# Layer 3's cross attention: query weights multiplied into the context's keys, scores taken straight from the tokens

## The chip, the cores and the metric

The kernel runs on one core of one Trainium2 chip. The metric is the device time of one launch in microseconds (us). The core has a matrix engine (TensorE, "PE" in the profile, with its weight loads as "PEld"), a vector engine (VectorE, "DVE"), a scalar engine (ScalarE, "ACT"), a general engine (GpSimd, "POOL") and an engine that issues most DMAs (SyncE, "SP"). Six runs of the kernel before took 2142.23 to 2151.93 us, median 2146.32 us.

## The reference, cut to what matters

A decoder of four layers; each layer adds self attention, cross attention to a short context, and a feed-forward block with experts to the tokens `x` (4 batches, 512 tokens, width 128), each on the layer-normed tokens. The context `ctx_1024` has 77 rows of width 128 in each of the 4 batches and is the same in all layers. The change is in the cross attention of the last layer, which has 16 heads of 64:

```python
def _L3_xattn_ref(query, key, value, w_q, w_k, w_v, w_o):
    HEADS = 16
    HEAD_DIM = 64
    scale = HEAD_DIM ** (-0.5)
    q = (query @ w_q).reshape(B, Q, HEADS, HEAD_DIM).transpose(0, 2, 1, 3)
    k = (key @ w_k).reshape(B, Kl, HEADS, HEAD_DIM).transpose(0, 2, 1, 3)
    v = (value @ w_v).reshape(B, Kl, HEADS, HEAD_DIM).transpose(0, 2, 1, 3)
    scores = jnp.einsum('bhqd,bhkd->bhqk', q, k) * scale
    attn = jax.nn.softmax(scores, axis=-1)
    out = jnp.einsum('bhqk,bhkd->bhqd', attn, v)
    out = out.transpose(0, 2, 1, 3).reshape(B, Q, HEADS * HEAD_DIM)
    return out @ w_o

x = x + _L3_xattn_ref(_layernorm(x), ctx_1024, ctx_1024, L3_xattn_w_q, L3_xattn_w_k, L3_xattn_w_v, L3_xattn_w_o)
x = x + _L3_ffn_ref(_layernorm(x), ...)
```

The weights `w_q`, `w_k` and `w_v` are 128 x 1024 and `w_o` is 1024 x 128. All products are in f32.

## The kernel before, in words

The tokens stay on chip all the time: `x` by rows (16 tiles of 128 tokens x 128), and `xT`, the normed tokens turned (128 x 2048), of which `tokens(b)` is a batch's 512 columns and `tile_of(t)` one tile's 128 columns. The stages follow one another, and beside the experts of a layer (much matrix work) the attention of the next is worked on: `weave(dense, chain, every)` writes the steps of a generator `dense` and after each `every` of them one step of a generator `chain`. What is written first has priority. A planner then sets, when the kernel is built, the order of each engine's instructions from its own cost model; engines named in `manual_schedule` keep the written order. Queues run in that order, each engine waiting for the semaphores of its own next instruction. Each f32 product shows as two matrix instructions in the trace, a transpose as one.

Cross attention of layer 3 has three parts.

*The context's part*, `l3_context` (L2215), depends on no token and is worked out early, in turns (`turns`, L408) with the second half of layer 0's experts (`ffn("l0_ffn", second, ...)`, 18 steps), while the chain beside them does layer 1's attention for batches 0 and 1 and its router (66 steps, one for each 0.48 dense steps, after a lead of 3). `l3_context` has 17 steps: one that loads the weights for keys, values and output (512 KB each, pool `x3c`), then two for each of eight pairs of heads `hp`. The first computes the pair's keys (128 x 308: two heads of 64 on the partitions, 4 x 77 context rows) and its values, each in a PSUM bank of the tag `f` (four banks, shared with the experts) and copied out by ACT; two DMAs store the keys in DRAM (`kd`). The second multiplies the values by `w_o`, head by head, and stores 77 x 512 for each head (`vd`). So values carry `w_o` already.

*The fetch*, `l3_keys` (L2246), is called inside the end of layer 3's self attention (`last`, L2109, where the order on PE, DVE, ACT and POOL is the written one). It clears a tile `kb` of 128 x (8 pairs, 4 batches, 2 heads, 77) with a POOL memset, since the two heads of a pair must not mix, and loads each head's keys into its own 64 partitions; the other 64 stay zero. It also loads the values `vo`.

*The main part*, `l3_xattn` (L2260), runs over 32 items (batch b, pair hp) in four phases, written one after the other with lags of 0, 1, 4 and 3 items (`lagged`, L418): `projections` (the pair's queries for the batch's 512 tokens, copied out by ACT with the factor 0.125), `scores`, `values`, `turn`. `scores` makes two PSUM tiles of one bank each, for two token tiles each: for a token tile it multiplies the 128 queries by the pair's keys with their zeros, 154 columns. Then for each of the two tiles: maximum, subtraction, sum and reciprocal on DVE, `exp` on ACT, and the multiplication by the reciprocals on POOL. `turn` transposes finished blocks of 128 (head, row) columns (10 blocks for the 8 pairs, 4 transposes each), ACT copies them out, and `values` multiplies each by `vo` into the batch's sum. PSUM banks: five of the tag `mm` (queries, scores and transposes take turns), two `acc`, one `s`.

Beside it the chain does the norms of batches 1 to 3 and, for batches 0, 1 and 2 in turn, `add_columns`, the norm and the router of layer 3's experts (`route_slots`, L759). POOL keeps the written order here: after each of POOL's multiplications in `scores`, `put` (L807) issues a waiting indirect DMA that sends 128 tokens to their expert's slots; for batch 3's items the second multiplication is followed by two. 16 such puts belong to each of three batches. What is left of them is put after the items, and the slots' experts follow.

The query weights come through `feed`, the list of weight packs that are loaded one after the other into four slots (`want`, `pack`): the pack `l3_xattn.q` stands between layer 2's experts and layer 3's.

Of the kernel before, what the change touches and what calls it, by code (L numbers as in the profile page):

```python
# [13 lines left out]
F32 = mybir.dt.float32  # L14
# [8 lines left out]
P = 128  # L23
B, S, D = 4, 512, 128
NT = B * S // P
TB = S // P
L = 77
# [103 lines left out]
def pack_all(inp):  # L131
    f32 = np.float32
    packs = {}


    p = packs["const"] = Pack()
# [15 lines left out]
    c, s = np.cos(ang).astype(f32), np.sin(ang).astype(f32)  # L152
# [5 lines left out]
    p = packs["l0_attn.qk"] = Pack()  # L158
    w, bias = inp["L0_attn_W_attn"], inp["L0_attn_b_attn"]
# [6 lines left out]
    p = packs["l0_attn.vo"] = Pack()  # L166
# [88 lines left out]
    for n in ("Wq", "Wk", "Wv"):  # L255
        p.add(n, inp["L3_attn_" + n].T)

    for n in "kvq":
        packs[f"l3_xattn.{n}"] = Pack()
        packs[f"l3_xattn.{n}"].add(n, inp["L3_xattn_w_" + n])  # L260
    packs["l3_xattn.o"] = Pack()
    packs["l3_xattn.o"].add("o", inp["L3_xattn_w_o"].reshape(8, P, D).transpose(1, 0, 2))

    p = packs["s5"] = Pack()
    p.add("gate_bias", rep(inp["L3_ffn_bias"]))
# [24 lines left out]
class Net:  # L290
# [1924 lines left out]
    def l3_context(self, pool):  # L2215

        nc = self.nc
        Wk, Wv, Wo = (self.load("l3_xattn." + n, pool, "x3" + n) for n in "kvo")
        kd = self.away.tile([2, 64, 8, B, L], F32, name="x3_k")
        vd = self.away.tile([16 * L, B, D], F32, name="x3_vo")  # L2220
        self.x3 = kd, vd
        yield
        for hp in range(8):
            c = slice(hp * P, hp * P + P)
            pk = self.bank("f", (P, B, L))
            self.dot(pk.rearrange("p b l -> p (b l)"), (Wk["k"][:, c], self.const["ctxT"]))
            k = pool.tile([P, B, L], F32, tag="x3kT", name="x3kT", bufs=2)
            nc.scalar.copy(k, pk)
            for h in range(2):
                nc.sync.dma_start(kd[h, :, hp], k[64 * h : 64 * h + 64])  # L2230
            pv = self.bank("f", (P, B * L))
            self.dot(pv, (Wv["v"][:, c], self.const["ctxT"]))
            vT = pool.tile([P, B * L], F32, tag="x3vT", name="x3vT", bufs=2)
            nc.scalar.copy(vT, pv)
            yield
            vo = pool.tile([L, 2, B, D], F32, tag="x3vo", name="x3vo", bufs=2)
            heads = [(h, slice(64 * h, 64 * h + 64), self.bank("f", (P, B, D))) for h in range(2)]
            for b in range(B):
                for h, r, po in heads:
                    self.dot(po[:L, b, :], (vT[r, b * L : b * L + L], Wo["o"][r, c]))  # L2240
            for h, r, po in heads:
                nc.scalar.copy(vo[:, h], po[:L])
            nc.sync.dma_start(vd[2 * hp * L : 2 * (hp + 1) * L].rearrange("(h l) b d -> l h b d", l=L), vo)
            yield

    def l3_keys(self, pool):  # L2246


        kd, vd = self.x3
        kb = pool.tile([P, 8, B, 2, L], F32, name="kb")  # L2250
# [9 lines left out]
    def l3_xattn(self, base, pool):  # L2260

        nc, tc = self.nc, self.tc
        HP = 8
        Wq = self.pack(base, "l3_xattn.q")
        kb, vo = self.x3
        items = [(b, hp) for b in range(B) for hp in range(HP)]
        made = {}
        accs = {}  # L2270
        rows = [(r, min(r + P, 16 * L)) for r in range(0, 16 * L, P)]

        blocks = [[i for i, (_, r) in enumerate(rows) if (r - 1) // (2 * L) == hp] for hp in range(HP)]

        def projections(b, hp):
            c = slice(hp * P, hp * P + P)
            pq = self.mm()
            self.dot(pq, (Wq["q"][:, c], self.tokens(b)))
            q = pool.tile([P, S], F32, tag="q", name="q", bufs=3)
            nc.scalar.mul(q, pq, 0.125)  # L2280
            made[b, hp, "q"] = q

        def scores(b, hp):
            q = made.pop((b, hp, "q"))
            es = []
            for j0 in range(0, TB, 2):
                s = self.mm((P, 4, L))
                for j in range(2):
                    self.dot(
                        s[:, 2 * j : 2 * j + 2, :].rearrange("p h l -> p (h l)"),  # L2290
                        (q[:, (j0 + j) * P : (j0 + j + 1) * P], kb[:, hp, b].rearrange("p h l -> p (h l)")),
                    )
                es.append(s)
            if hp == 0:
                made[b, "e"] = pool.tile([P, TB, 16, L], F32, tag="heads", name="heads", bufs=2)
            for i, s in enumerate(es):
# [4 lines left out]
                nc.vector.tensor_reduce(m, s, AX.X, ALU.max)  # L2301
                self.tt(e, s, wide(m), ALU.subtract)
                nc.scalar.activation(e, e, AF.Exp)
                nc.vector.tensor_reduce(r, e, AX.X, ALU.add)
                nc.vector.reciprocal(r, r)
                nc.gpsimd.tensor_tensor(e, e, wide(r), ALU.mult)
                if (b, hp) not in items[-2:]:
                    self.put(2 if i and b == B - 1 else 1)

        def turn(b, hp):  # L2310
            e = made[b, "e"].rearrange("p j h l -> p j (h l)")
            for i in blocks[hp]:
                r0, r1 = rows[i]
                t = self.mm((P, TB, P))
                for j in range(TB):
                    nc.tensor.transpose(t[: r1 - r0, j, :], e[:, j, r0:r1], self.ident)
                eT = pool.tile([P, S], F32, tag="eT", name="eT", bufs=4)
                nc.scalar.copy(eT[: r1 - r0], t[: r1 - r0].rearrange("l j q -> l (j q)"))
                made[b, i] = eT

        def values(b, hp):
            if hp == 0:
                accs[b] = self.acc()
            for i in blocks[hp]:
                n = rows[i][1] - rows[i][0]
                nc.tensor.matmul(  # L2326
                    accs[b], lhsT=vo[:n, i, b, :], rhs=made.pop((b, i))[:n], start=i == 0, stop=i == len(rows) - 1,
                )
# [24 lines left out]

def build(nc, packs, dram):
# [9 lines left out]
    at = {}  # L2364
    for name, part in (
        ("l0a", of("l0_ffn")), ("l0b", of("l0_ffn")), ("l1a", of("l1_ffn")), ("l1b", of("l1_ffn")),
        ("l2", f2 + one_by_one), ("x3", ["l3_xattn.q"]), ("l3", of("l3_ffn")[:3]),
    ):
        at[name] = len(feed)
        feed += part  # L2370
    with tile.TileContext(nc) as tc, ExitStack() as ctx:
# [102 lines left out]
        close_pool("f2")  # L2474


        net.want(at["x3"])
# [11 lines left out]
        x3 = open_pool("x3")  # L2489
        banks(mm=5, acc=2, s=1)  # L2490
        w5 = net.load("s5", s5, "w")
        steps = net.l3_xattn(at["x3"], x3)

        class Both(dict):
            def __missing__(self, name):
# [66 lines left out]
```

## Time and profile before

| what | value |
|---|---|
| median of six runs | 2146.32 us |
| profiled execution, its own time | 2143.78 us |
| span of its trace | 2142.1 us, mean granted TensorE clock 0.983 |
| PE / DVE / ACT / POOL busy in the span | 95% / 74% / 46% / 28% |
| context's part, first keys to last values stored | 303.7 to 395.8 us |
| main part, first query product to last sum copied out | 1887.5 to 2033.5 us |

A view by lines gives, for a line of the code, an engine and an operation, how many instructions there were and their durations. A view by windows gives for each stretch of time how long each engine was busy, the number of its instructions, the share of full speed that the TensorE clock was granted (PEclk), and the mean busy share of the 16 DMA engines. The chain of waits follows the work that ended last backwards; on it the pitch of matrix instructions can be read, which is shorter than the duration of one, since they are pipelined.

### The profile page before, as it was taken

The page shows a single profiled execution, that of the slowest core. Times are in us where ns is not written, and L with a number is a line of the kernel's source. Part 1 is how long each engine was busy: PE and PEld are TensorE (multiplying, and loading weights), DVE is VectorE, ACT ScalarE, POOL GpSimd, SP SyncE. Part 2 cuts the span into 40 slices and gives each one's busy share as a digit, 9 for nine tenths or more (in the row PEclk, how much of TensorE's full clock was granted, in tenths as well). Part 3 has the DMA queues.
Part 4 walks back from the last instruction along what each step waited for, and adds up shares of the span by engine and source line. Part 5 has one row for each costly group of instructions (what it writes and reads, how often), then busy time and mean ns, then how long its engine had stood idle before and what let it go on. Part 6 is the DMA issues. An engine that isn't in the chain of part 4 may idle for free.

```text
span 2142.1 us, 27766 instructions
## 1 busy us (share of the span) xinstructions
PE 2032.2 (95%) x8804; PEld 1065.9 (50%) x8804; DVE 1593.2 (74%) x3932; ACT 990.1 (46%) x2023; POOL 594.2 (28%) x778
## 2 busy tenths in 40 slices
PE   6989999999999999999999999999999999899886
PEld 3555546554545453444444544444444444466553
DVE  6788675756765779778977798777866877599755
ACT  4556546444325462534543454434433544267541
POOL 2110101000000001433333243332432355145753
PEclk8999999999999999999999999999999999999988
DMA  6421443344453343333333444444454354431112
GB/s 161 122 78 47 107 113 101 93 130 112 116 133 91 90 110 98 86 103 97 104 105 106 111 112 126 123 129 120 125 137 117 99 142 124 96 97 39 32 43 82
DMA packets 93985, 222.56 MB, mean 104 GB/s; under 512 B 22178, under 2 KB 43106, under 8 KB 93582
## 3 DMA queue, kind: packets, MB, share of 16 engines
q1 hardware_dynamic: 90702, 218.63, 37.7%
q0 software_dynamic: 3136, 2.16, 0.4%
q8 instruction: 69, 1.13, 0.2%
q14 instruction: 78, 0.64, 0.1%
HBM read 192.55 MB, written 23.53 MB: 101 GB/s over the span
## 4 chain that ended last, share of the span: by engine, by line
PE 60%; DVE 13%; ACT 3%; issue 3%; POOL 2%; DMA 1%; another core or an unknown queue 0%; SPq 0%; DVEq 0%; POOLq 0%; ACTq 0%
PE mm L431 17%; PE f L431 11%; PE mm L1874 8%; PE s L431 6%; PE mm L1846 5%; PE acc L1039 5%; PE mm L1821 4%; DVE h L442 1%; DVE at_m L1907 1%; ACT at_e L1909 1%; DVE gvx L442 1%; PE acc L2326 1%; DVE k_work L442 1%; DVE og L442 1%; PE acc L1077 1%
## 5 line engine op out<-in xcount | busy, mean ns | idle before, releaser
L1782 POOL TENSOR_TENSOR gvx<-gvx 128x512 f32<-128x512 f32 (+1 forms) x256 | 262.9, 1027 | 529.9 <-DVE gvx L442 471.5
L431 PE MATMUL f<-xT,w_l_ffn 128*128 128x512 f32 (+1 forms) x700 | 334.9, 599 | 1.3 <-ACT h L1031 0.7
L1909 ACT ACTIVATE at_e<-mm,at_m 128x512 f32<-128x512 f32 x256 | 173.1, 686 | 265.0 <-DVE at_m L1907 259.6
L431 PE MATMUL mm<-w_l_ffn_qkv,xT 128*128 128x512 f32 x512 | 264.4, 602 | 3.3 <-DVE gvx L442 1.7
L1874 PE MATMUL mm<-og,w_l_ffn_o 128*128 128x512 f32 x512 | 263.2, 600 | 2.8 <-DVE og L442 1.4
L442 DVE TENSOR_TENSOR h<-h,f 128x512 f32<-128x512 f32 (+1 forms) x175 | 119.5, 685 | 120.7 <-PE f L431 95.9
L1031 ACT ACTIVATE h<-f 128x512 f32<-128x512 f32 x172 | 102.2, 596 | 211.7 <-PE f L431 188.1
L442 DVE TENSOR_TENSOR gvx<-mm,gv 128x512 f32<-128x512 f32 x256 | 174.2, 684 | 23.9 <-PE mm L431 20.0
L442 DVE TENSOR_TENSOR og<-mm,c 128x512 f32<-128x512 f32 x256 | 174.0, 682 | 22.8 <-PE mm L1874 21.0
L431 PEld LDWEIGHTS f<-xT,w_l_ffn 128*128 128x128 f32 (+1 forms) x700 | 125.7, 190 | 130.2 <-issue 107.4
L1039 PE MATMUL acc<-h,w_l_ffn 128*128 128x512 f32 x344 | 176.8, 597 | 4.9 <-DVE h L442 3.6
L1907 DVE TENSOR_REDUCE at_m<-mm 128x1 f32<-128x512 f32 x256 | 161.2, 682 | 11.8 <-PE mm L431 11.2
L1822 ACT COPY eT<-mm 128x512 f32<-128x512 f32 x256 | 137.3, 595 | 68.3 <-PE mm L1821 68.0
L1821 PEld LDWEIGHTS mm<-ident,at_e 128*128 128x128 f32 x1024 | 119.4, 141 | 66.5 <-issue 45.4
L1874 PEld LDWEIGHTS mm<-og,w_l_ffn_o 128*128 128x128 f32 x512 | 91.3, 190 | 114.6 <-issue 90.5
L1821 PE MATMUL mm<-ident,at_e 128*128 128x128 f32 x1024 | 134.7, 273 | 3.3 <-ACT at_e L1909 3.3
L431 PEld LDWEIGHTS mm<-w_l_ffn_qkv,xT 128*128 128x128 f32 x512 | 86.9, 190 | 91.5 <-issue 54.5
L431 PE MATMUL mm<-roped 64*128 64x512 f32 x512 | 129.4, 615 | 1.6 <-DVE roped L442 1.6
L1846 PE MATMUL mm<-eT,v 128*64 128x512 f32 x512 | 118.5, 598 | 2.1 <-ACT eT L1822 2.1
L442 DVE TENSOR_TENSOR h<-h,c 128x512 f32<-128x512 f32 x160 | 111.2, 700 | 3.3 <-DMA c<-l_ffn_w 0.4
L1248 ACT ACTIVATE e<-mm 128x512 f32<-128x512 f32 (+1 forms) x176 | 92.1, 554 | 42.9 <-PE mm L1244 39.0
L1202 DVE TENSOR_REDUCE m<-mm 128x1 f32<-128x512 f32 (+3 forms) x176 | 102.5, 625 | 9.5 <-PE mm L1198 8.8
(528 smaller groups left out, 3485.0 us busy)
## 6 DMA issues: line engine op xcount, KB each, us to landing
c<-gates SPq DMA_DIRECT2D x256, 256.0 KB
c<-l_ffn_w SPq DMA_DIRECT2D x96, 384.0 KB
w_l_ffn_qkv<-in_l_ffn_qkv SPq DMA_DIRECT2D x24, 640.0 KB
w_l_ffn<-in_l_ffn SPq DMA_DIRECT2D x26, 576.0 KB
w_l_ffn_o<-in_l_ffn_o SPq DMA_DIRECT2D x24, 512.0 KB
rot<-qk SPq DMA_DIRECT2D x128, 64.0 KB
d<-inverted SPq DMA_DIRECT2D x64, 128.0 KB
k_parts<-k SPq DMA_DIRECT2D x12, 384.0 KB
```

Source lines behind the costliest of these rows:

```text
L431: self.nc.tensor.matmul(out, lhsT=lhsT, rhs=rhs, start=i == 0, stop=i == len(pairs) - 1)
L442: self.nc.vector.tensor_tensor(out, a, b, op)
L1031: nc.scalar.activation(h, pg, AF.Silu)
L1039: nc.tensor.matmul(acc["t"], lhsT=W["d" + u], rhs=h, start=i == 0, stop=i == n - 1)
L1202: nc.vector.tensor_reduce(m[:, i, h0 : h0 + per], ps, AX.X, ALU.max, negate=True)
L1782: nc.gpsimd.tensor_tensor(x[:, :, :m], x[:, :, :m], x[:, :, m : 2 * m], ALU.add)
L1821: nc.tensor.transpose(p[:, j, :], es[i][hl][:, j * P : j * P + P], self.ident)
L1822: nc.scalar.copy(eT[hl][:, :, i * P : i * P + P], p)
L1846: nc.tensor.matmul(po[64 * hl : 64 * hl + 64, :], lhsT=m["v"][:, j, hl, :], rhs=eT[hl][:, j, :], start=j == 0, stop=j == TB - 1,)
L1874: nc.tensor.matmul(acc, lhsT=W["o"][:, (e - 1) * D : e * D], rhs=hs.pop(e - 1), start=e == 1, stop=e == E)
L1907: nc.vector.tensor_reduce(m, s, AX.X, ALU.max, negate=True)
L1909: nc.scalar.activation(e[:, :n], s, AF.Exp, bias=m, accum_out=den)
```

## The change

Scores are q k^T = x (w_q k^T), so the query weights can be multiplied into the keys, once for all tokens. The change does so in the context's part. The query weights are packed by head dimension (1024 rows in 8 blocks of 128), loaded in `l3_context` between those for keys and values, and no longer in `feed`. The keys are copied out with the factor 0.125; a new step multiplies, for each of the pair's two heads, the head's 64 rows of `w_q` (transposed) by the head's keys (128 x 308 in an `f` bank), ACT copies both into one tile, and one DMA stores them. `l3_context` has 25 steps in place of 17. The stored keys are 128 rows deep for each head and not 64: `kd` and the loads from it move 2.52 MB and not 1.26 MB, in four DMAs of 4,928 bytes a partition and not two of pieces of 308 bytes; the memset is gone. In `l3_xattn` the phase `projections` is gone, `scores` multiplies `tile_of` by `kb`, and the lags and the weave's numbers are set for three phases.

```diff
     def l3_context(self, pool):
-        Wk, Wv, Wo = (self.load("l3_xattn." + n, pool, "x3" + n) for n in "kvo")
-        kd = self.away.tile([2, 64, 8, B, L], F32, name="x3_k")
+        Wk, Wq, Wv, Wo = (self.load("l3_xattn." + n, pool, "x3" + n) for n in "kqvo")
+        kd = self.away.tile([B, P, 8, 2, L], F32, name="x3_k")
...
-            k = pool.tile([P, B, L], F32, tag="x3kT", name="x3kT", bufs=2)
-            nc.scalar.copy(k, pk)
-            for h in range(2):
-                nc.sync.dma_start(kd[h, :, hp], k[64 * h : 64 * h + 64])
+            kT = pool.tile([P, B * L], F32, tag="x3kT", name="x3kT", bufs=2)
+            nc.scalar.mul(kT, pk, 0.125)
...
+            yield
+            k = pool.tile([P, B, 2, L], F32, tag="x3kx", name="x3kx", bufs=2)
+            heads = [(h, slice(64 * h, 64 * h + 64), self.bank("f", (P, B, L))) for h in range(2)]
+            for h, r, pk in heads:
+                self.dot(pk.rearrange("p b l -> p (b l)"), (Wq["q"][r, c], kT[r]))
+            for h, r, pk in heads:
+                nc.scalar.copy(k[:, :, h, :], pk)
+            nc.sync.dma_start(
+                kd[:, :, hp].rearrange("b p h l -> p b (h l)"), k.rearrange("p b h l -> p b (h l)")
+            )
             yield
...
     def l3_keys(self, pool):
-        kb = pool.tile([P, 8, B, 2, L], F32, name="kb")
+        kb = pool.tile([P, B, 8, 2, L], F32, name="kb")
...
-        self.nc.gpsimd.memset(kb, 0.0)
-        for h in range(2):
-            self.nc.sync.dma_start(kb[64 * h : 64 * h + 64, :, :, h, :], kd[h])
+        for b in range(B):
+            self.nc.sync.dma_start(kb[:, b], kd[b])
...
     def l3_xattn(self, pool):
-        def projections(b, hp):
-            c = slice(hp * P, hp * P + P)
-            pq = self.mm()
-            self.dot(pq, (Wq["q"][:, c], self.tokens(b)))
-            q = pool.tile([P, S], F32, tag="q", name="q", bufs=3)
-            nc.scalar.mul(q, pq, 0.125)
-            made[b, hp, "q"] = q
...
-                        (q[:, (j0 + j) * P : (j0 + j + 1) * P], kb[:, hp, b].rearrange("p h l -> p (h l)")),
+                        (self.tile_of(TB * b + j0 + j), kb[:, b, hp].rearrange("p h l -> p (h l)")),
...
-        return self.lagged(items, (projections, 0), (scores, 1), (values, 4), (turn, 3))
+        return self.lagged(items, (scores, 0), (values, 3), (turn, 2))
...
-        ("l2", f2 + one_by_one), ("x3", ["l3_xattn.q"]), ("l3", of("l3_ffn")[:3]),
+        ("l2", f2 + one_by_one), ("l3", of("l3_ffn")[:3]),
...
-            net.weave(some(steps, 40), chained(net.norm(1), net.empty_slots(s5), net.norm(2), net.norm(3)), 2.5)
+            net.weave(some(steps, 28), chained(net.norm(1), net.empty_slots(s5), net.norm(2), net.norm(3)), 1.75)
             w5.gate = net.load("s5.gate", s5, "wg")
-            net.weave(some(steps, 32), chain5(0), 1.3, ahead=300)
+            net.weave(some(steps, 24), chain5(0), 0.97, ahead=300)
             net.want(at["l3"] + 1)
-            net.weave(some(steps, 32), chain5(1), 1.3, ahead=300)
-            net.weave(steps, chain5(2), 0.85, ahead=300)
+            net.weave(some(steps, 24), chain5(1), 0.97, ahead=300)
+            net.weave(steps, chain5(2), 0.71, ahead=300)
```

More of the change, by code (lines that the diff above doesn't have):

```diff
@@ L256, in pack_all @@
         p.add(n, inp["L3_attn_" + n].T)
-    for n in "kvq":
+    for n, w in (
+        ("k", inp["L3_xattn_w_k"]), ("v", inp["L3_xattn_w_v"]),
+        ("q", inp["L3_xattn_w_q"].T.reshape(8, P, D).transpose(1, 0, 2)),
+        ("o", inp["L3_xattn_w_o"].reshape(8, P, D).transpose(1, 0, 2)),
+    ):
         packs[f"l3_xattn.{n}"] = Pack()
-        packs[f"l3_xattn.{n}"].add(n, inp["L3_xattn_w_" + n])
-    packs["l3_xattn.o"] = Pack()
-    packs["l3_xattn.o"].add("o", inp["L3_xattn_w_o"].reshape(8, P, D).transpose(1, 0, 2))
+        packs[f"l3_xattn.{n}"].add(n, w)
     p = packs["s5"] = Pack()
@@ L2224, in l3_context @@
             c = slice(hp * P, hp * P + P)
-            pk = self.bank("f", (P, B, L))
-            self.dot(pk.rearrange("p b l -> p (b l)"), (Wk["k"][:, c], self.const["ctxT"]))
-            k = pool.tile([P, B, L], F32, tag="x3kT", name="x3kT", bufs=2)
-            nc.scalar.copy(k, pk)
-            for h in range(2):
-                nc.sync.dma_start(kd[h, :, hp], k[64 * h : 64 * h + 64])
+            pk = self.bank("f", (P, B * L))
+            self.dot(pk, (Wk["k"][:, c], self.const["ctxT"]))
+            kT = pool.tile([P, B * L], F32, tag="x3kT", name="x3kT", bufs=2)
+            nc.scalar.mul(kT, pk, 0.125)
             pv = self.bank("f", (P, B * L))
@@ L2258, in l3_keys, with l3_xattn @@
         self.x3 = kb, vo
-    def l3_xattn(self, base, pool):
+    def l3_xattn(self, pool):
         nc, tc = self.nc, self.tc
         HP = 8
-        Wq = self.pack(base, "l3_xattn.q")
         kb, vo = self.x3
@@ L2273, in l3_xattn @@
         blocks = [[i for i, (_, r) in enumerate(rows) if (r - 1) // (2 * L) == hp] for hp in range(HP)]
-        def projections(b, hp):
-            c = slice(hp * P, hp * P + P)
-            pq = self.mm()
-            self.dot(pq, (Wq["q"][:, c], self.tokens(b)))
-            q = pool.tile([P, S], F32, tag="q", name="q", bufs=3)
-            nc.scalar.mul(q, pq, 0.125)
-            made[b, hp, "q"] = q
         def scores(b, hp):
-            q = made.pop((b, hp, "q"))
             es = []
@@ L2474, in build @@
         close_pool("f2")
-        net.want(at["x3"])
         x3c, a3b = open_pool("x3c"), open_pool("a3b")
@@ L2491, in build @@
         w5 = net.load("s5", s5, "w")
-        steps = net.l3_xattn(at["x3"], x3)
+        steps = net.l3_xattn(x3)
         class Both(dict):
```

## The prediction

> **What bounds the kernel now.** The change touches two stages, so I read those, first by windows, then for waits. The first table is from layer 0's experts with the context's part beside them, the second from the main part. Columns: stretch, its length, then busy us (and instructions) of PE, PEld, DVE, ACT and POOL, granted clock, DMA share, GB/s.
>
> ```profile
> 320.00:340.00 20.00, 20.00 (x125) 14.66 (x124) 10.48 (x25) 15.73 (x30) 2.75 (x4) 1.00 0.36 100
> ...
> 360.00:380.00 20.00, 19.22 (x116) 13.49 (x115) 10.85 (x41) 8.98 (x18) 1.41 (x2) 1.00 0.18 54
> ```
> ```profile
> 1949.00:1964.00 15.00, 15.00 (x76) 10.13 (x75) 13.89 (x49) 8.58 (x18) 6.27 (x8) 1.00 0.02 6
> ...
> 1994.00:2009.00 15.00, 12.90 (x63) 8.12 (x62) 13.76 (x50) 7.93 (x19) 13.12 (x16) 1.00 0.02 3
> ```
>
> Work is moved into a stage where PE has next to no gap, out of one where PE is full but DVE is over 90% full too, and from 1994 on POOL as well. So PE time added counts in full; PE time removed counts only as far as DVE and POOL let it. The waits of the main part (engine and line, what it waited for: us in all, times, longest) say how far:
>
> ```profile
> DVE fits L724 <- PE s L431: 3.0, 2, 2.8
> DVE sm_s L2304 <- ACT heads L2303: 2.7, 8, 0.5
> ...
> DVE sm_m L2301 <- PE mm L431: 2.1, 4, 0.8
> ...
> DVE x L442 <- PE s L462: 1.8, 2, 1.3
> ```
>
> DVE hardly ever waits for the scores (sm_m, 2.1 us in 146); further down the same answer has 1.1 for the router's sigmoid (sb). For POOL I read its timeline; around an item of batch 3 (start, duration, idle before in brackets):
>
> ```profile
> 2005.45 0.72 POOL L2306 TENSOR_TENSOR heads<-heads,sm_s 128x308 f32<-128x308 f32 x1
> 2006.34 1.00 POOL L801 DMA_INDIRECT slots<-sent,to  x1 [0.17 <-issue]
> 2007.37 0.71 POOL L2306 TENSOR_TENSOR heads<-heads,sm_s 128x308 f32<-128x308 f32 x1
> 2008.25 1.00 POOL L801 DMA_INDIRECT slots<-sent,to  x1 [0.17 <-issue]
> 2009.55 0.97 POOL L801 DMA_INDIRECT slots<-sent,to  x1 [0.30 <-issue]
> ```
>
> From 1995.29 to 2020.75 this pattern (2 multiplications, 3 puts, 5.1 us) runs five times with no idle time but issue gaps: items 25 to 29 go at POOL's pace. Items 17 to 24, one put to a multiplication, take 35.3 us (1960.01 to 1995.29) where 16 x (0.72 + 1.0 + 0.2) = 31 us is POOL's least. Only items 0 to 16 (1893.82 to 1960.01, 3.9 us each) are free of puts.
>
> **What a matrix instruction costs** is its pitch, not its duration. From the chain of waits and PE's timeline:
>
> ```profile
> 1919.29 1.91 PE mm L431 x10
> 1921.20 0.86 PE acc L2326 x2
> 1922.06 0.87 PE mm L2316 x8
> ```
> ```profile
> 389.87 0.68 PE L431 MATMUL f<-w_const,w_l_xattn_k 128*128 128x308 f32 x2
> 390.39 0.68 PE L431 MATMUL f<-w_const,w_l_xattn_v 128*128 128x308 f32 x2
> ...
> 393.58 1.10 PE L431 MATMUL f<-w_l_xattn_o,x3vT 64*77 64x128 f32 x16
> 394.61 3.21 PE L431 MATMUL f<-xT,w_l_ffn 128*128 128x512 f32 x6
> ```
>
> 512 columns: 0.43 us; 308: 0.52 / 2 = 0.26; 128: 0.109; ten with two query instructions: 1.91 - 0.86 = 1.05 for eight of scores. With 64 rows in turns of two heads, 16 of 128 columns start to start in 1.03: 0.064 each, 0.59 of 0.109, so the heads' halves overlap.
>
> **Part 1, the new product in the context's part.** Per pair two products of 64 rows and 308 columns, four instructions, 32 in all. At the full-row pitch: 32 x 0.26 = 8.3 us. If all overlap as the values do: x 0.59 = 4.9. Here a head's two instructions stand together and only the second of one can meet the first of the other: three of four pitches, 8 x 0.78 = **+6.2** (4.9 to 8.3). It lies on PE, with nothing to hide it.
>
> **Part 2, copies, banks and steps.** 16 more ACT copies of 128x308 at 0.416 us (the row of the key copies) = 6.7 us, hidden while ACT is under 80% busy. Each needs an `f` bank until ACT has come; queued behind it on ACT are the experts' silu copies, and PE waits for both. The waits of PE over 300 to 440 us sum to 1.7 us in all, so the margin is thin. The context's steps also outnumber the experts' by more: 25 against 18, and the last seven (2.3 pairs, about 6.6 us of ACT copies) stand alone behind the chain, whose 66 steps end at dense step 35 of 43; layer 1's experts must fill in. I take **+1.5**, between 0 (filled) and 4 (most of the 6.6 seen).
>
> **Part 3, DMAs and queues, costed at 0.** The keys' stores: 8 of 308 KB in pieces of 616 bytes for 16 of 77 KB; DMA is at 0.18 to 0.36 there, SP issues eight fewer. The query weights' load moves from 1811 to about 252 us, ahead of the values' and output's on SP (issued to 262); first use is 303.7, and 512 KB at the 100 GB/s of that stage is 5 us. The memset (4.2 us) leaves POOL, which after it idles 5.4 us for ACT: worth nothing itself, but the fetch no longer waits for it. The fetch has 2.52 MB + 2.46 MB of values from 1828 on; at 160 GB/s it lands by 1860, first use 1887. That cover gone, it would be a stall of up to 16 us for the keys.
>
> **Part 4, the main part.** Removed: 64 query instructions x 0.43 = 27.3 us of PE and 32 x 0.595 = 19.0 of ACT. PE per item falls from 0.86 + 1.05 + 1.25 x (0.44 + 0.86) = 3.5 to 2.7 us. What DVE can get back is its waits for PE and ACT: sm_m 2.1 + x 1.8 + sm_s 2.7 + sb 1.1 = 7.7, less 1.5 after 1995 where POOL sets the pace: 6.2 at most. Waits behind ACT's exp and the norm's transposes remain, so I take half: **-3** (0 to -6.2). POOL's stretch: **0**. The start: first maximum at 1890.58, first query product 1887.54, a score product takes 1.3; at most 1.8 comes free, but DVE is full with norms from 1887 to 1904 (14.79 busy of 15 from 1889), so **-0.5**.
>
> **Part 5, the tail and the clock.** From 2020.75 to the last sum out at 2033.5:
>
> ```profile
> 2016.00:2020.00 4.00, 2.06 (x11) 1.83 (x11) 3.84 (x22) 2.83 (x7) 3.35 (x5) 0.69 0.90 279
> 2020.00:2024.00 4.00, 4.00 (x16) 3.37 (x17) 1.33 (x6) 0.65 (x2) 2.20 (x4) 0.50 0.37 140
> ```
>
> After a stretch with PE about half busy (2.06 of 4) the clock is half, and stays 0.53 to 2028, and DVE then waits 2.8 us for the router's small products (fits, above). With 0.86 of 5.1 us less to do per item, PE is emptier in POOL's stretch; half clock may start earlier, but fewer value products queue up. **0** (-3 to +3). Sum: 6.2 + 1.5 - 3 - 0.5 = **+4.2** on the profiled execution, 2143.8 to 2148.0. The median of the runs stands 2.5 above that execution, so the forecast is **2150.5**.
>
> A rule speaks against the change here. The Trainium skill, "TensorE: Matmul & The Clock Gate", section "Why this matters for your kernels", asks for no PE gap over about 3 us, or the clock falls to half. The trace shows half clock after gaps of at most 1.7 us, so on this point the measurement is harsher than the rule. By the rule the main part, whose gaps should stay under 2 us, keeps its clock, the tail could give 3 us back and the forecast would be 2147.5.
>
> **Rivals.** *Faster:* DVE gets all its waits back and the tail shrinks: -6.2 - 1.8 - 3 against +4.9: 2140. For it: ACT is rid of 19 us, and five `mm` banks serve fewer tiles, so scores run ahead. Against: DVE's own 92 to 93%, and POOL's stretch. *Slower, the clock:* PE drops under the share of work that holds the clock all through the main part. An item needs 2.7/g us at clock g; the pitch of items 0 to 24 is 101.5/25 = 4.06, so it decides below g = 0.66. At 0.60 it is 4.5 x 25 = 112.5, 11 us more, with parts 1 and 2: 2146.3 + 7.7 + 11 = 2165; at 0.62, 2160. For it: the rows above. Against: 1.00 at 12.90 of 15 busy. *Slower, the banks:* the four `f` banks and ACT hold PE up for the last seven steps: 6.6 more, 2157. *The change does not do what it says:* the 27 us leave PE and the main part is as long: parts 1 and 2 alone, 2154; I count it to the forecast.
>
> **How the numbers follow.** Low: 4.9 - 6.2 - 1.8 - 3 = -6.1 to 2140.2; high: 8.3 + 4 + 3 = 15.3 to 2161.6. Forecast 0.45, faster 0.2, clock 0.15, banks 0.2. A change under 0.3% (6.4 us) can't be told from none. Faster: most of that rival, 0.2 with a little of the forecast. Slower: clock 0.13, banks 0.14, and 0.13 of the forecast's upper end. The rest is no difference. The range of 2139.5 to 2161.5 leaves out the clock's worse half and a little below.
>
> **What would show it.** Step 1: 32 rows of products from the query weights and keys, 0.6 to 1.0 us for four. Step 2: PE's waits between 300 and 440 us, and the time from the first key product to the end of layer 1's router. Step 4: DVE above 95% busy to 1955, item pitch 3.7. POOL's five items unchanged at 25.4 us. Clock under 0.9 in 1900 to 2000 would speak for the clock rival. I am wrong altogether if the planner orders the stages differently elsewhere, or if the fetch is late.

## The result, and the profile after

The changed kernel takes 2160.33 us (median of 22 runs, 2148.96 to 2169.25) where the kernel before takes 2147.69 on the same chip: a ratio of 1.0057, 95% interval 1.0042 to 1.0071, or +12.2 us. A second set gave 1.0055 (1.0033 to 1.0076), +11.7 us. A copy of the kernel before, timed in the same way, came out at 0.9969 (0.9951 to 0.9986), so such an interval leaves out some 0.3% that a set of runs can be off by; the loss is about twice that.

The windows of the changed kernel's two stages: stretch, length, then busy us (instructions) of PE, PEld, DVE, ACT and POOL, granted clock, DMA share, GB/s. The first two rows are layer 0's experts, the others the main part from its first score maximum to batch 1's sum, and from there to batch 3's.

```profile
320.00:340.00 20.00, 19.76 (x114) 13.46 (x113) 9.76 (x32) 14.46 (x29) 2.75 (x4) 1.00 0.34 93
...
400.00:420.00 20.00, 17.38 (x94) 9.79 (x91) 12.12 (x42) 9.44 (x21) 1.07 (x2) 1.00 0.65 179
...
1905.10:1971.80 66.70, 59.20 (x315) 40.42 (x313) 64.10 (x250) 41.29 (x87) 26.65 (x40) 1.00 0.25 80
1971.80:2050.00 78.20, 61.78 (x284) 39.74 (x282) 60.07 (x230) 37.32 (x75) 59.23 (x75) 0.87 0.15 46
```

The kernel before, the last of the stage's stretches and the same halves of the main part:

```profile
400.00:420.00 20.00, 19.91 (x60) 9.29 (x58) 18.13 (x82) 5.64 (x11) 0.80 (x2) 1.00 0.44 107
...
1890.60:1961.20 70.60, 67.67 (x350) 46.42 (x349) 64.17 (x239) 51.19 (x106) 26.66 (x41) 1.00 0.24 76
1961.20:2033.50 72.30, 64.52 (x308) 42.57 (x306) 58.56 (x225) 43.18 (x87) 59.24 (x75) 0.93 0.16 50
```

The stage of layer 0's experts now has a stretch with 2.6 us of empty PE. The main part's first half is 3.9 us shorter: DVE does the same 64.1 us in 66.7 instead of 70.6. Its second half is 5.9 us longer, with PE less busy and a lower clock. What the first half gains, the second loses, and the key product is paid on top.

The halves don't hold quite the same work, since the planner's order differs between the two kernels. When batch 1's sum is copied, 36 of the 64 score maxima are done in the changed kernel and 38 in the kernel before; DVE has done more of the norms instead. In the second half it then has 1.5 us more to do (60.07 against 58.56).

DVE's waits in the first half, before and after (engine and line, what it waited for: us in all, times, longest):

```profile
DVE sm_s L2304 <- ACT heads L2303: 1.6, 5, 0.4
DVE x L442 <- PE s L462: 1.3, 1, 1.3
DVE none_rows L841 <- POOL none_rows L839: 0.9, 1, 0.9
DVE sb L442 <- ACT sig L594: 0.8, 1, 0.8
DVE sm_m L2301 <- PE mm L431: 0.8, 2, 0.6
```
```profile
DVE sm_s L2303 <- ACT heads L2302: 1.9, 4, 0.8
```

5.6 us with a last row of 0.2 not shown became 1.9; the 3.7 between them is nearly all of the 3.9.

**One profile misleads at the end.** The two profiled executions differ by 22.8 us (spans 2164.9 and 2142.1), of which 6.2 lie behind the main part. But the copy of the kernel before had a span of 2152.6: from 2036 us on, in identical code, it fell 10.5 us behind the first profile. From the copy of the last sum, the tail was 109 to 122 us long in all profiles taken on chips where before takes 2148 to 2154, and 95 to 98 where it takes 2131, with no order by kernel. So I compare three things: the whole times by ratio, and within the profiles two stages that repeat.

- Layer 0's stage: how much matching DVE and ACT instructions shift against the first profile of before from 250-300 to 520-600 us.
- The main part: the first score maximum to the copy of each batch's sum.

```
kernel             time, ratio (95%)         layer 0's   sums of batches 1, 3   clock after
                                             stage, us   (us from 1st maximum)  batch 1
before             1                          0           70.6   142.9           0.93
copy of before     0.9969 (0.9951-0.9986)    +0.8         70.6   142.8           0.93
keys_alone         1.0039 (1.0021-1.0057)   +10.3         70.6   142.5           0.95
scores_alone       0.9995 (0.9977-1.0014)    +0.4         66.7   143.6           0.90
changed            1.0057 (1.0042-1.0071)    +8.2         66.7   144.9           0.87
changed, again     1.0055 (1.0033-1.0076)    +8.3         66.7   143.7           0.90
filled             1.0051 (1.0033-1.0070)   +10.2         68.5   141.0           0.95
two_steps          1.0057 (1.0035-1.0079)   +14.4         66.7   143.5           0.90
even_steps         1.0077 (1.0049-1.0105)   +12.8         66.7   143.6           0.90
act_half           1.0046 (1.0024-1.0069)   +11.2         66.7   143.7           0.87
late_keys          1.0005 (0.9986-1.0025)    -0.1         63.9   143.8           0.91
late_filled        1.0027 (1.0011-1.0043)    -0.1         69.6   144.5           0.93
```

### The profile page after: what moved, and what is told of

The parts are those of the page before. It is cut to its first block, busy times and chain, and to the rows that moved or that the text cites. A ratio compares the mean times of both kernels' runs of the same rounds, so it can differ in the third digit from the quotient of the medians.

```text
span 2164.9 us, 27667 instructions
## 1 busy us (share of the span) xinstructions
PE 2039.4 (94%) x8772; PEld 1067.6 (49%) x8772; DVE 1594.8 (74%) x3932; ACT 979.2 (45%) x2007; POOL 590.3 (27%) x777
## 4 chain that ended last, share of the span: by engine, by line
PE 68%; DVE 19%; ACT 4%; issue 3%; DMA 3%; POOL 2%; SPq 0%; another core or an unknown queue 0%; DVEq 0%; ACTq 0%; POOLq 0%
PE mm L433 17%; PE f L433 13%; PE mm L1876 8%; PE s L433 8%; PE acc L1041 5%; PE mm L1848 5%; PE mm L1823 4%; DVE h L444 2%; PE mm L1262 2%; DVE x L444 1%; DVE st L495 1%; PE mm L1197 1%; DVE at_m L1909 1%; PE s L527 1%; PE mm L1242 1%
```

## The experiments

**1. Each half alone.** `keys_alone` is the kernel before with the new product beside layer 0's experts; the old keys are stored and used as before.

```diff
+        kx = self.away.tile([B, P, 8, 2, L], F32, name="x3_kx")
...
+            for h, r, pk in heads:
+                self.dot(pk.rearrange("p b l -> p (b l)"), (Wq["p"][r, c], k.rearrange("p b l -> p (b l)")[r]))
+            for h, r, pk in heads:
+                nc.scalar.copy(kk[:, :, h, :], pk)
```

> The kernel before with the query weights multiplied into the keys in the context's part (loads, steps, copies and an extra store as in the changed kernel), but with the old main part, which goes on making queries. Theory A, the loss is paid where work is put: the stage of layer 0's experts grew by 8.2 us in the profile, nothing comes back, so +8 us over the kernel before, about 0.4%. Theory B, most of the loss arises in the main part through an emptier TensorE: at most +4 us here, and the rest shows in the kernel with the scores alone. The clock in the main part stays 1.00 up to 2010 us by both.

`scores_alone` has the new main part with the old context and fetch; it leaves out the query weights.

```diff
-                        (q[:, (j0 + j) * P : (j0 + j + 1) * P], kb[:, hp, b].rearrange("p h l -> p (h l)")),
+                        (self.tile_of(TB * b + j0 + j), kb[:, hp, b].rearrange("p h l -> p (h l)")),
...
-        return self.lagged(items, (projections, 0), (scores, 1), (values, 4), (turn, 3))
+        return self.lagged(items, (scores, 0), (values, 3), (turn, 2))
```

> The main part of the changed kernel (scores straight from the tokens, three phases) with the context's part and the fetch of the kernel before. Left out: the query weights; the scores are made of tokens and plain keys, with the same shapes and counts. The prediction's own part 4: -3.5 us against the kernel before. Theory B, the emptier TensorE loses its clock from about 2000 us on, and the value products and the next stage's start pay: between 0 and +5 us, with a granted clock under 0.85 between the main part's 100th and 150th us, where the kernel before has 1.00 until 20 us before the end.

The keys alone cost 8.4 us (0.39%), the scores alone gain 1.1 (0.05%, the interval holds zero). Theory A is right about the place of the loss, B about the main part: its first half gains 3.9 us and its second gives 4.6 back. The two add up to 7.3 of the measured 12; the intervals, some 4 us to each side, don't tell that apart from the whole.

**2. Is it the emptier PE?** `filled` is the changed kernel plus a product that nobody reads, where the queries were.

```diff
         def scores(b, hp):
             es = []
+            idle = self.mm()
+            self.dot(idle, (kb[:, b, hp].rearrange("p h l -> p (h l)")[:, :P], self.tokens(b)))
```

> The changed kernel with one more product for each of the 32 items, 128 columns of the keys with the tokens into a bank that nobody reads: 0.43 us of TensorE for an item, 13.8 us in all, in the place where the queries were. Theory B, an emptier TensorE loses its clock: the clock stays at 0.95 or more up to the end of GpSimd's stretch, and the time is 3 to 8 us under the changed kernel's (2152 to 2157 where that has 2160). Rival C, the clock costs nothing there because DVE and GpSimd set the pace: the same time within 2 us. Rival D, the added product lies on the path: +5 us or more.

With 13.8 us of useless work added, the main part is 2.7 to 3.9 us shorter than in the changed kernel: batch 1's sum comes 1.8 later, but from there to batch 3's it takes 72.5 us instead of 77.0 or 78.2, about what before takes (72.3):

```profile
1977.70:2050.20 72.50, 63.64 (x310) 42.05 (x308) 57.71 (x224) 37.15 (x75) 56.50 (x72) 0.95 0.16 50
```

The time as a whole doesn't show it: +11.0 us to +12.2, in two sets, so by the times rival C came true, not theory B. This filled execution had 2 us more in layer 0's stage, and the intervals are some 4 us to each side. Nor is the fill the only difference: with it the planner chose another order, with 38 score maxima done at batch 1's sum as in the kernel before, and DVE has 2.4 us less to do behind it (57.71 against 60.07). The run alone can't tell the clock from the order.

The clock of the part is shown in four windows of 4 us at the same place, first the changed kernel, then the filled one:

```profile
1994.00:1998.00 4.00, 4.00 (x29) 3.28 (x28) 3.99 (x18) 1.44 (x3) 3.60 (x5) 1.00 0.01 0
1998.00:2002.00 4.00, 2.10 (x9) 1.02 (x8) 4.00 (x11) 0.66 (x2) 2.38 (x3) 1.00 0.01 0
2002.00:2006.00 4.00, 2.86 (x12) 2.42 (x13) 3.38 (x12) 2.27 (x5) 2.05 (x3) 0.57 0.01 0
2006.00:2010.00 4.00, 4.00 (x11) 2.15 (x10) 1.93 (x6) 0.07 (x1) 3.61 (x5) 0.58 0.01 0
```
```profile
1998.00:2002.00 4.00, 4.00 (x21) 2.71 (x21) 3.12 (x17) 1.21 (x3) 3.48 (x4) 1.00 0.01 0
2002.00:2006.00 4.00, 4.00 (x22) 2.80 (x21) 3.79 (x12) 1.42 (x4) 1.47 (x2) 1.00 0.01 0
2006.00:2010.00 4.00, 3.71 (x19) 2.27 (x18) 3.46 (x11) 2.23 (x5) 3.02 (x5) 1.00 0.01 0
2010.00:2014.00 4.00, 4.00 (x20) 2.46 (x19) 3.01 (x12) 1.75 (x4) 3.54 (x5) 1.00 0.01 0
```

In the changed kernel PE is busy 2.10 of 4 us, and then has little over half its clock for 8 us: the two rows lose 3.4 us, that is 6.8 us at half clock. Its timeline says what emptied it (start, duration, in brackets the idle time before and who ended it):

```profile
1999.97 0.41 PE L2315 MATMUL mm<-ident,heads 128*128 128x128 f32 x2
2002.40 0.58 PE L2315 MATMUL mm<-ident,heads 128*128 128x128 f32 x2 [2.03 <-POOL heads L2305]
```

The transposes wait for POOL's multiplication, as they did before; but there are no queries to do meanwhile, and such waits of PE add up to 14.0 us in the part where they were 4.4. While the clock is low DVE is idle for more than half of a window (1.93 busy of 4), its work comes late, and POOL waits for it, in the middle of the puts:

```profile
2009.83 1.00 POOL L803 DMA_INDIRECT slots<-sent,to  x1 [0.17 <-issue]
2013.54 0.69 POOL L2305 TENSOR_TENSOR heads<-heads,sm_s 128x308 f32<-128x308 f32 x1 [2.70 <-DVE mv L496]
```

That this drop lengthens the part is shown by profiles in which PE, DVE and ACT run the same instructions in the same order up to there, as far as the traces name them (but for a few at the end, of batch 3, in act_half and act_scale). Each of the seven with this new first half has the 2.03 us gap and a drop behind it. In two of them (changed, act_half) the drop lasted 6.8 us, and batch 2's sum came 105.3 and 105.4 us after the first maximum. In the other five (changed again, scores_alone, two_steps, even_steps, act_scale) it lasted 3.4 us, and the sum came at 103.7 to 103.8: 1.5 to 1.7 us sooner, for 1.7 us less of lost clock. The second profile of the changed kernel around its drop:

```profile
1990.50:1995.50 5.00, 4.50 (x16) 3.51 (x17) 4.24 (x14) 2.13 (x5) 3.13 (x5) 0.67 0.01 0
```

The clock isn't the whole of it. POOL's first multiplication of each item, taken from the first maximum and set against the kernel before (items counted from 0; us, minus is sooner), tells where the lead goes:

```
item                16     18     22     24     26     31    batch 3's sum
changed            -6.4   -2.2   -1.7   -0.8   +1.7   +0.6   +2.1
changed, again     -6.4   -2.2   -1.7   -0.9   +0.2   -0.4   +0.8
filled             -1.6   -2.5   -2.0   -1.3   -1.3   -1.3   -1.8
```

The lead falls from 6.4 to 2.2 us by item 18 and to under 1 by item 24, all at full clock. Between items 16 and 18 DVE does 10.7 us of work other than the softmax there, against 2.1 in the kernel before: the time gained went into work of the chain done sooner. The first drop comes between items 24 and 26 and costs 1.1 or 2.5 us there. The last 1.2 to 1.5 us go between item 31 and the last sum. There a gap of PE of 2.94 us (again for POOL) is followed by half clock, and the last products of the values run in it, while in the kernel before the half clock is over by 2028. The changed kernel's rows:

```profile
2042.00:2046.00 4.00, 1.44 (x5) 0.98 (x6) 1.43 (x5) 1.14 (x3) 2.17 (x4) 0.69 0.00 0
2046.00:2050.00 4.00, 3.46 (x4) 0.84 (x3) 0.00 (x0) 0.61 (x2) 3.45 (x7) 0.50 0.02 1
```

**3. Is it POOL's pace?** `act_half` lets ScalarE make the first of batch 3's two multiplications of an item.

```diff
-                nc.gpsimd.tensor_tensor(e, e, wide(r), ALU.mult)
+                if b == B - 1 and i == 0:
+                    for j in range(2):
+                        for h in range(2):
+                            nc.scalar.mul(e[:, j, h, :], e[:, j, h, :], r[:, j, h : h + 1])
+                else:
+                    nc.gpsimd.tensor_tensor(e, e, wide(r), ALU.mult)
```

> The changed kernel, but of batch 3's two multiplications of an item the first is made by ScalarE (four of 77 columns, 1.1 us together), the second stays on GpSimd between the puts. GpSimd then needs 0.72 + 3 x 1.27 = 4.5 us for an item instead of 5.1. Theory F, its pace holds the main part's end: 2 to 4 us off the time from the first maximum to the last sum (143.5 to 144.9), to 140 to 142. Rival, the puts run ahead of the adds that VectorE waits for, as with all the multiplications taken away (156.7): longer than 145.

POOL's item fell to 4.4 us, as wanted (timeline of POOL, three items' multiplications):

```profile
2007.21 0.70 POOL L2310 TENSOR_TENSOR heads<-heads,sm_s 128x308 f32<-128x308 f32 x1 [3.61 <-DVE sm_s L2304]
...
2011.62 0.72 POOL L2310 TENSOR_TENSOR heads<-heads,sm_s 128x308 f32<-128x308 f32 x1
...
2016.07 0.72 POOL L2310 TENSOR_TENSOR heads<-heads,sm_s 128x308 f32<-128x308 f32 x1
```

The last score maximum then came 122.2 us after the first, where the changed kernel has 133.5 and 134.5; yet the last sum came at 143.7, no sooner. Theory F falls: POOL's pace alone isn't what the part ends on. In act_half's own waits from 2010 on, POOL waits 7.1 us for one sum of DVE, and DVE 4.6 for the router's small products (`fits`), with 0.50 of the clock from 2028 to 2038. That fits a part that ends on the low clock, but no run holds the clock up there by itself. With all 16 multiplications on ScalarE:

> The changed kernel, but batch 3's 16 multiplications by the reciprocal sums are made by ScalarE (four of 77 columns for each) instead of GpSimd, which is left with the puts. Theory F, GpSimd's 5.1 us for each of the last items is what the main part ends on: three puts take 3.5 us, VectorE's own work 3.7, so 4 to 6 us under the changed kernel. Rival: the clock at half speed and ScalarE's own 3.4 us for an item take its place: the changed kernel's time within 2 us.

That took 1.0085 (1.0059 to 1.0110) and the part 156.7 us. With no multiplication between them, the puts on POOL ran one after another, and DVE stood still for 15.9 us, ahead of an add onto x. It tells nothing of theory F, only that the multiplications also space the puts; that the puts held the add up is likely, not shown. The same edit on the kernel of experiment 5 did the same (1.0098, 1.0076 to 1.0119; part 161.8 us); its expectation was

> Both edits, the keys' product in the main part and batch 3's multiplications on ScalarE. By theories E and F together: 5 to 10 us under the kernel before, 2138 to 2143 where that has 2148. By their rivals: within 3 us of the kernel before, or slower.

**4. The steps that stand alone.** The key product in the same step as keys and values (`two_steps`, one yield less), and layer 1's chain spread over the whole stage (`even_steps`):

```diff
             nc.scalar.copy(vT, pv)
-            yield
             k = pool.tile([P, B, 2, L], F32, tag="x3kx", name="x3kx", bufs=2)
```

> The changed kernel with the key product in the same step as the keys and values: 17 steps in the context's part for the experts' 18, so none stands alone behind them. Prediction's part 2, the lone steps cost the wait of 2.6 us for the weights' halves: 2 to 3 us under the changed kernel. Rival: the new product needs the step between to wait for its key copy; TensorE then waits about 0.5 us in each of 8 pairs, and the time is the changed kernel's or up to 4 us more.

```diff
-            chained(net.l1_context(s2, w2), chain2(first)), 0.48, 3,
+            chained(net.l1_context(s2, w2), chain2(first)), 0.6, 3,
```

> The changed kernel with layer 1's chain spread over all 43 dense steps of layer 0's stage (one chain step to 0.6 dense steps instead of 0.48), so that the context's last steps don't stand alone behind it. Prediction's part 2, the lone steps make the wait of 2.6 us for the weights' halves: the wait goes, layer 0's stage is 2 to 4 us shorter than in the changed kernel (5 to 6 us over before's), the rest as there. Rival: the chain, whose end the next stage needs, only comes later, and layer 1's experts wait for it: the stage as long or longer.

The wait that was PE's longest in the changed kernel's stage, there, in two_steps and in even_steps:

```profile
PE s L677 <- POOL w_halves L670: 2.6, 1, 2.6
```
```profile
PE s L677 <- POOL w_halves L670: 0.4, 1, 0.4
```
```profile
PE s L677 <- POOL w_halves L670: 0.8, 1, 0.8
```

The wait shrank, as expected, and the stage grew all the same, to +14.4 and +12.8 us: in both runs the rival came true. Even_steps in windows, with the gap that begins it:

```profile
366.15 0.78 PE L433 MATMUL f<-x3kT,w_l_xattn_q 64*128 64x308 f32 x2
368.00 1.32 PE L554 MATMUL s<-ident,sm_e 128*77 128x128 f32 x8 [1.07 <-POOL sm_e L547]
```
```profile
360.00:370.00 10.00, 8.78 (x28) 3.90 (x26) 4.10 (x11) 6.45 (x13) 1.35 (x2) 0.98 0.28 91
370.00:380.00 10.00, 10.00 (x28) 6.55 (x28) 2.46 (x8) 1.59 (x3) 0.00 (x0) 0.50 0.10 32
380.00:390.00 10.00, 10.00 (x70) 8.57 (x69) 5.45 (x24) 0.78 (x2) 0.00 (x0) 0.84 0.00 0
```

Behind a gap of 1.07 us PE is busy without a break, at half the clock, for some 13 us: 5.0 + 1.6 us lost in the last two rows. Taken off, the stage is 12.8 - 6.6 = 6.2 us longer than before's. Two_steps has two gaps of 0.73 and 0.45 us at the same place, ahead of these rows:

```profile
370.00:380.00 10.00, 10.00 (x48) 8.65 (x47) 2.46 (x8) 1.17 (x2) 0.00 (x0) 0.55 0.00 0
380.00:390.00 10.00, 9.87 (x57) 7.01 (x56) 7.41 (x40) 4.81 (x12) 0.00 (x0) 0.93 0.24 71
```

They lose 5.2 us; without them its stage would still be 9.2 longer, so two_steps has another loss, which wasn't looked for. The lone steps do make the wait (part 2's mechanism), and moving them opened smaller gaps elsewhere, with half clock behind them. In the kernels left with the 2.6 us wait, it cost only itself in three profiles (changed, changed again, act_scale: +8.2 to +8.5), and a low clock behind it in three others (keys_alone, filled, act_half: +10.2 to +11.2). In keys_alone, where the clock is under 1 only here:

```profile
403.50:407.50 4.00, 1.78 (x14) 1.37 (x15) 2.64 (x6) 0.65 (x2) 0.64 (x1) 0.95 0.70 201
407.50:411.50 4.00, 4.00 (x18) 2.65 (x16) 0.00 (x0) 1.89 (x4) 0.00 (x0) 0.62 0.66 172
```

**5. The product where PE has room.** `late_keys` fetches the scaled plain keys and makes the product in the main part, in batch 0's eight items, ahead of their scores.

```diff
+        self.nc.sync.dma_start(kT, kd.rearrange("h p n -> p h n"))
...
+        def keys(b, hp):
+            if b:
+                return
+            heads = [(h, slice(64 * h, 64 * h + 64), self.mm((P, B, L))) for h in range(2)]
+            for h, r, pk in heads:
+                self.dot(
+                    pk.rearrange("p b l -> p (b l)"), (Wq["q"][r, hp * P : hp * P + P], kT[r, hp, :])
+                )
+            for h, r, pk in heads:
+                nc.scalar.copy(kb[:, :, hp, h, :], pk)
...
+        return self.lagged(items, (keys, 0), (scores, 1), (values, 4), (turn, 3))
```

> The query weights multiplied into the keys in the main part instead of beside layer 0's experts: in batch 0's eight items two products of 64 rows and 308 columns each, and two copies on ScalarE, ahead of the item's scores; the plain keys (scaled, half the bytes) are fetched with no zeroing. Theory E, the main part has 13.8 us of TensorE to spare (the filled kernel lost nothing by them), the stage of layer 0's experts has none: the 8 to 10 us of that stage come back and the time is that of the scores alone, -4 to +1 us against the kernel before. Rival: batch 0's items stand at the start of the main part, where the norms hold VectorE, and five banks serve two more tiles an item; the scores then come late: +3 to +8.

Layer 0's stage is as before (-0.1 us) and the time is that of the kernel before (+1.1 us, at the edge of the -4 to +1 expected; the interval holds zero): theory E holds as far as the times can tell. That undoes the loss, and shows that it came from where the product was put; it brings no gain, because the main part still ends at 143.8. Filling that kernel up from batch 1 on (the two lines of experiment 2 under `if b:`) was to bring the gain:

> The query weights multiplied in the main part (late keys), and from batch 1 on one product of 128 columns of the keys with the tokens for each item, which nobody reads: 24 x 0.43 = 10.3 us of TensorE. If the filled kernel's main part (141.0 us from the first maximum to the last sum) came from the clock held up, this one has 141 to 142 where the late keys alone have 143.8, layer 0's stage as before, and ends 1 to 4 us under the late keys, -4 to 0 us against the kernel before. Rival: the added products only lengthen the main part, to 144 or more.

It did not: 144.5 us, 0.27% over before, which is what the rival said. The half after batch 1's sum did shrink, from 79.9 to 74.9, but the one before it grew by 5.7. The clock behind batch 1's sum rose only from 0.91 to 0.93, some 2 us less lost, for 10.3 us of added products. So useless work is no remedy, and filled's shorter part isn't put down to the clock alone. No version tried beats the kernel before.

**6. The two kernels again.**

> The kernel before, unchanged, for a second profile of it. If the gains and losses of whole microseconds that several profiles share against the first profile of before in code that none of them changes (1.9 us at 860 us, 1.4 at 1310 to 1460, 7 to 9 at 2036 to 2045) are that one execution's luck, this one shows them too, with a ratio of 1.000 within 0.2%. If they belong to the changed kernels, it runs like the first profile.

> The changed kernel, unchanged, for a second profile and a second set of times. If the stages are what decides: from the first score maximum to the last batch's sum 143.5 us as in the scores alone and the two steps, or 144.9 as in the first profile, against 142.5 to 142.9 in three profiles with the old main part; layer 0's stage 8 to 10 us longer than before's; the time +9 to +15 us against the kernel before. If the first profile was its own luck: main part under 142, or a time within 6 us of before.

The copy of before showed the 7.4 us at 2036 to 2045 and 1.1 of the 1.4 at 1310 to 1460, so these are no work of the change; of the 1.9 at 860 it showed next to nothing, and neither did the second profile of the changed kernel, so that one stays unexplained. It was off by 0.31%, more than the 0.2% I allowed. The changed kernel's second profile has the stages of the first within 0.1 us, but for a drop of the clock in batch 2 (1.5 us less at its sum, 1.2 at the end).

## Why the prediction was right or wrong

The time lies within the range, near its upper end: 2150.5 was forecast (+4.2 us, 0.2%), +12 came. It is slower by more than the 0.3%, which had 4 chances in 10, as had no difference. That the range held is in part its width: the loss is three times the one forecast.

- **Part 1, the product: right in size, in part by luck.** It said 6.2 us, by 0.78 for four instructions. The changed kernel's timeline has (the last column tells how many instructions stand together)

```profile
309.24 0.79 PE L433 MATMUL f<-x3kT,w_l_xattn_q 64*128 64x308 f32 x4
309.96 1.12 PE L433 MATMUL f<-xT,w_l_ffn 128*128 128x512 f32 x2
...
322.22 0.78 PE L433 MATMUL f<-x3kT,w_l_xattn_q 64*128 64x308 f32 x2
322.93 0.44 PE L527 MATMUL s<-ident,xn 128*128 128x128 f32 x2
...
399.15 0.79 PE L433 MATMUL f<-x3kT,w_l_xattn_q 64*128 64x308 f32 x4
399.78 1.04 PE L433 MATMUL f<-w_l_xattn_o,x3vT 64*77 64x128 f32 x16
```

  Four together take 0.72 or 0.63 from start to start, less than 0.78. But they stand together in five pairs of eight only. In the others the two instructions of one head stand alone and take 0.71, more than the 0.52 of two full-row ones. With 1.1 for the pair that the 2.6 us wait splits, that makes an estimated 7.4 us: the two errors partly cancel.
- **Part 2, copies, banks and steps: right in size where the clock stayed up.** It said 1.5, of at most 4. PE's waits in the stage (300 to 452 us) went from 2.3 us in all to 3.8, so +1.5; with part 1 that is 8.9, where the stage grew by 8.2. Half clock behind the wait, in three profiles of six, made it 10.2 to 11.2; the sum had no term for that. The wait isn't one for banks or ScalarE, as the rival had it, but for the router's chain on DVE and POOL, with the context's steps used up too early.
- **Part 3, transfers and queues: right at 0.** In the main part neither profile of the changed kernel has a wait for the keys.
- **Part 4, the main part: right up to batch 1, but the gain didn't last.** It said -3.5 with the start; 3.9 us were gained by then, DVE 96% busy (64.10 of 66.70) where over 95 was to be seen. By item 18 only 2.2 us of the lead were left and by item 24 under 1, at full clock. DVE's waits were gained, but the time went into work of the chain done sooner (10.7 us against 2.1 between items 16 and 18), which didn't bring the last sum forward. The items of POOL's stretch kept their 5.1 us:

```profile
2016.67 0.73 POOL L2305 TENSOR_TENSOR heads<-heads,sm_s 128x308 f32<-128x308 f32 x1
...
2021.76 0.72 POOL L2305 TENSOR_TENSOR heads<-heads,sm_s 128x308 f32<-128x308 f32 x1
```

- **Part 5, the clock at 0: this step failed.** It set an earlier half clock off against fewer value products. From batch 1's sum to batch 3's the changed kernel takes 77.0 and 78.2 us against 72.3, so +4.7 to +5.9, outside its -3 to +3. Of that, 2.3 to 3.9 us come up to batch 2's sum, where the kernel before had a full clock and the drop loses 1.7 or 3.4; the other 2.0 to 2.4 come behind it, with the last products at half clock; how much of these 2.0 to 2.4 is the clock was not measured. The clock rival had the mechanism, but asked for a clock under 0.66 throughout from item 0 on and 11 us; it was 1.00 until 2000 us, and a few drops of 3.4 to 7 us each were enough to take away what was left of the gain.

The sum by what was measured in profiles: the stage 8.2 and the main part 144.9 - 142.9 = 2.0 make 10.2 us in the first profile of the changed kernel, 8.3 + 0.8 = 9.1 in the second, and 11.2 + 2.0 = 13.2 where the clock is unlucky in both. The 11.7 and 12.2 of the times lie in that. What share of executions is unlucky was not measured.

## What to carry to other kernels

Work moved off an engine counts only as far as another engine was waiting for it; here that was 3.7 us of DVE's waits for 27 us of TensorE, and not even these were kept to the end. Before moving it, ask where the receiving stage has room: the same product cost 8 us beside a full TensorE, and nothing that the times can tell where VectorE set the pace. And work taken off TensorE in a stage where it waits for others makes its gaps longer; price the clock that those gaps cost, in every batch, and compare stages over several profiles before explaining a tail. Where a planner sets the order, a run that adds work changes the order too: compare how far each engine has come, and not only when a batch ends.

## What the runs showed of the hardware

- Half clock came after single gaps of TensorE of 2.03 us (main part, in all seven profiles that have it) and 1.07 us (even_steps), after two of 0.73 and 0.45 us (two_steps), and a gap of 2.62 us was followed by it in three profiles of six. The Trainium skill, "TensorE: Matmul & The Clock Gate", section "Why this matters for your kernels", asks for no gap over about 3 us; all of these are shorter, so the measurement decides. No run here settles what else it goes by.
- A low clock lasted 3.4 or 6.8 us after the 2.03 us gap, in the same code, and about 13 us in even_steps, though TensorE had no break in it there (10.00 busy of 10, at 0.50). The longer of the first two made batch 2's sum 1.5 to 1.7 us later.
- With useless work on TensorE, and another order of VectorE's work, the rest of the main part was 4.5 to 5.7 us shorter (filled, against the changed kernel's two profiles), with a clock of 0.95 instead of 0.87 and 0.90; in late_filled it brought no gain (144.5 against 143.8).
- Stages of one kernel repeat to some 0.1 us from one execution to the next where the clock does (batch 1's sum 66.7 us in seven kernels and profiles, on different chips), while the last 100 us differ by 10 in identical code. Why they do wasn't tried.
